# Rows for two products: turned as 16-bit planes by DMA instead of by TensorE

## The chip, the cores and the metric

The kernel runs on one core of a Trainium2 chip. A core has five engines that run side by side, each with its own list of instructions: TensorE (PE) multiplies matrices, VectorE (DVE), ScalarE (ACT) and GpSimd (POOL) work on tiles of 128 partitions, and SyncE (SP) issues transfers (DMA) between DRAM and the on-chip memory, SBUF. TensorE writes its results to a small memory of its own, PSUM, from which DVE or ACT fetch them. An engine works its list in order; where it needs what another engine or a transfer makes, it waits on a semaphore, and everything behind it in its list waits too. ACT and POOL can issue transfers as well.

The metric is the device time of one execution in microseconds (us), smaller is better. It is given as the median of several runs. The profile shows one further execution.

## The reference

A graph of N = 2708 nodes with a feature row of D = 512 numbers each goes through four layers, each followed by `x = layernorm(x + layer(x))`. `adj` is the 2708 x 2708 matrix of edges. Cut to the layers that the change touches:

```python
# layer 0: mean over the first 64 neighbours of every node
keep = Ab & (cumsum(Ab, axis=1) <= 64)
nb_mean = (keep @ X) / max(cnt, 1)
x = layernorm(X + leaky(X @ W_line.T + b_line) + where(cnt > 0, leaky(nb_mean @ W_nb.T + b_nb), 0))
# layer 1: mean over all neighbours
agg = mask @ x / max(deg, 1)
x = layernorm(x + relu(concat([x @ W_self + b_self, agg @ W_nb + b_nb]) @ W_comb + b_comb))
# layer 2: attention with 8 heads; its projection:
Wh = einsum('ni,hio->hno', x, W)        # 512 -> 8 x 64
f1, f2 = Wh . a[:, :64], Wh . a[:, 64:]
# ... softmax over the neighbours, weighted sum of Wh
# layer 3: two more attentions of this kind and a feed-forward part
```

## The kernel before

The rows are worked in 22 tiles of 128 nodes; the last (`LAST`) has 20. The edges lie in SBUF for the whole run as `maskT`, one byte each, transposed, with a sign for kept and other neighbours.

A product `x @ W` on TensorE needs the left operand with the features in the partitions, so each tile of rows is transposed first. `transposed` (lines 132 to 139) does it: four TensorE transposes of 128x128 into one PSUM tile (line 136), and a copy by ACT to the SBUF tile `xT` (line 138). Tiles are drawn ahead of need by `early` (line 161): `early(first, n, make)` makes item i + first when item i is asked for. The row loads are `fetched` (line 174), issued on SP's queue into a ring of three buffers named `rows` in the pool `ahead`. That ring is shared by everything that fetches rows.

The stages that matter here, with the times of the profiled execution:

- 0 to 190 us: layer 0's two products for all tiles, and the first 14 tiles of masks.
- 190 to 455: layer 0's aggregation (lines 571 to 595). Six column blocks of up to four tiles, the short one first; in each, 22 steps in which ACT makes the operand `kT` from the mask (line 444) and TensorE adds into four PSUM banks (line 581). The mean over the neighbours is taken after the product with the weight, here and in layer 1, so `y = x W` is what is aggregated, kept as a high and a low part, `yH` and `yL`. At the end of a block ACT moves the sums out (line 594), and `finish` (lines 494 to 507), drawn a step at a time in the next block, completes the rows of x1: it loads layer 0's second product `r0` and the input row `x0` into `rows` buffers, applies bias, leaky relu and the sum (lines 498 to 504), then the layer norm, which is split between DVE (lines 118 to 125) and POOL (line 123), and stores the row tile to `x1_dram` from POOL's queue (line 506). Beside it the same loop draws steps of `other_masks` (lines 447 to 482: the last eight tiles of masks, each loaded, counted by ACT at line 288, placed by DVE's scans at lines 294 and 297, transposed by an SP transfer at line 315 and written to `maskT` by ACT at line 320), of `weights1` (layer 1's combined weights) and of `vectors` (line 546, the attention's vectors).
- 455 to 620: layer 1's first products (lines 600 to 618). For each tile: fetch the x1 rows, transpose, multiply by the neighbour weight, keep the result as `yH` by ACT (line 242) and `yL` by DVE (line 247), turn a slice of the mask to 0 and 1 by DVE (line 610), multiply by the own weight, add the bias by DVE (line 616), store to `z1_dram`. The steps of `finish` left from the last block are drawn here.
- 620 to 835: layer 1's aggregation (lines 621 to 638): per tile ACT casts mask slices (line 629), TensorE adds over all tiles (line 632), DVE and POOL complete the row of x2 (lines 635 to 637), and POOL's queue stores it (line 638).
- 835 to 927: layer 2's projection, `project` with `source = plain` (lines 705 to 815): per tile fetch the x2 rows, transpose, 16 products (line 759), and the small vectors for the attention that follows.

TensorE's order is that in which the program gives its instructions. On the other engines a planner orders the instructions by costs and due times; `tc.issue_after` holds an instruction behind another.

Of the kernel before, what the change touches and what calls it, by code (L numbers as in the profile page):

```python
# [10 lines left out]
F32 = mybir.dt.float32  # L11
F32R = mybir.dt.float32r
BF16 = mybir.dt.bfloat16
F8 = mybir.dt.float8e4
AF = mybir.ActivationFunctionType
OP = mybir.AluOpType
AX = mybir.AxisListType
# [2 lines left out]
P = 128  # L20
D = 512
KD = D // P
# [9 lines left out]
def kernel(  # L32
# [9 lines left out]
    nc = tc.nc  # L42
    N = x.shape[0]
    NT = -(-N // P)
# [6 lines left out]
    def rows(t):  # L51
        return min(P, N - t * P)
# [7 lines left out]
    dram = ctx.enter_context(tc.tile_pool(name="dram", bufs=1, space=bass.MemoryType.DRAM))  # L60
# [21 lines left out]

    maskT = big.tile([P, NT, NT * P], F8, name="maskT")
    r0_dram = dram.tile([N, D], F32, name="r0_dram")
    x1_dram = dram.tile([N, D], F32, name="x1_dram")
    z1_dram = dram.tile([N, D], F32, name="z1_dram")
    x2_dram = dram.tile([N, D], F32, name="x2_dram")
    x3_dram = dram.tile([N, D], F32, name="x3_dram")


    o_dram = dram.tile([N, D], F32, name="o_dram")
    oT_dram, rc_dram = [], []

# [2 lines left out]
    few = N - (NT - 1) * P  # L96
    LAST, TWIN = NT - 1, 32
# [18 lines left out]
    def layer_norm(pool, y, n, dst, on_scalar=False):  # L116
# [10 lines left out]
        nc.vector.scalar_tensor_tensor(mv[:n, 0:1], mv[:n, 0:1], -1.0, rs[:n], op0=OP.mult, op1=OP.mult)  # L127
        nc.scalar.activation(dst, y, AF.Identity, bias=mv[:n, 0:1], scale=rs[:n])

    copied = []  # L130

    def transposed(pool, psum, src, n, name, order=as_it_comes):

        ps = psum.tile([P, KD, P], F32, name="ps_tr")
        for k in range(KD):
            order(nc.tensor.transpose(ps[:, k, :n], src[:, k * P:(k + 1) * P], ident[:n, :n]))
        dst = pool.tile([P, KD, P], F32, name=name)
        copied[:] = [nc.scalar.copy(dst[:, :, :n], ps[:, :, :n])]  # L138
        return dst

    def transpose_weight(room, psum, dst, src, queues=(nc.sync,)):

# [10 lines left out]
    ahead = fast.enter_context(tc.tile_pool(name="ahead", bufs=2))  # L153
# [7 lines left out]
    def early(first, n, make):  # L161

        made = {}

        def get(i, **how):
            for j in range(len(made), min(i + first + 1, n)):
                made[j] = make(j, **how)
            return made[i]
        return get
# [4 lines left out]
    def fetched(src, t, n, pool=ahead, name="rows", bufs=None, log=None):  # L174
        x_ = pool.tile([P, D], F32, name=name, bufs=bufs or (3 if pool is ahead else None))
        ins = nc.sync.dma_start(x_[:n], src[t * P:t * P + n, :])
        if log is not None:
            log.append(ins)
        return x_[:n]
# [28 lines left out]
    with ExitStack() as phase:  # L208
# [19 lines left out]
        ps_tr = phase.enter_context(tc.tile_pool(name="ps_tr", bufs=2, space=PSUM))  # L228
# [3 lines left out]
        sm = phase.enter_context(tc.tile_pool(name="l01", bufs=2))  # L232
# [53 lines left out]
        def count(i, m):  # L286
            t, n = turns[i], rows(turns[i])
            nc.scalar.activation(m[:n, :N], m[:n, :N], AF.Sigmoid, bias=gate[:n], scale=STEP, accum_out=cnts[:n, t:t + 1])

# [9 lines left out]
        def turn_here(i, m, psum, order=as_it_comes):  # L299
            t, n = turns[i], rows(turns[i])  # L300
            for g0 in range(0, NT, G):
# [6 lines left out]
                for w, a, b in parts:  # L308
                    if a < b:
                        nc.scalar.activation(maskT[:w, a:b, t * P:t * P + n], ps[:w, a - g0:b - g0, :n], AF.Sign,  # L310
                                             saturate=False)
# [12 lines left out]
            b = min(b * P, N)  # L324
            nc.gpsimd.dma_start(maskT[TWIN:TWIN + few, LAST, a * P:b], maskT[:few, LAST, a * P:b])

        def rows_of(src):
            return early(2, NT, lambda t: fetched(src, t, rows(t)))

        with ExitStack() as ph:  # L330
            st = ph.enter_context(tc.tile_pool(name="l0a", bufs=1))
            wnT, wlT = weight(), weight2
            room = [maskT[:, G + k, :4 * D].bitcast(F32) for k in range(2 * KD)]
# [3 lines left out]
            fetches = []  # L337
            xs = early(2, NT, lambda t: fetched(x, t, rows(t), log=fetches))
            xTs = early(0, NT, lambda t, order=as_it_comes: transposed(ahead, ps_tr, xs(t), rows(t), "xT", order))

            warm = sums()
# [5 lines left out]
            xT = xTs(0, order=pe)  # L347
            lows[0] = keep_y(0, P, product(xT, P, wnT, 0, pe))
            xT = xTs(1, order=pe)
# [46 lines left out]
            for t in range(NT):  # L396
                n = rows(t)
# [8 lines left out]
                xT = xTs(t)  # L406
# [17 lines left out]
                u = sm.tile([P, D], F32, name="u")  # L424
# [12 lines left out]
        with ExitStack() as ph:  # L437
# [56 lines left out]
            def finish(ts_, us):  # L494
                for t in ts_:
                    n, u = rows(t), us[t]
                    r0, x0 = fetched(r0_dram, t, n), fetched(x, t, n)
                    nc.vector.tensor_add(u[:n], u[:n], b_nb[:n])
                    leaky(u[:n], u[:n])
                    with tc.issue_after(low.ins):  # L500
                        leaky(r0, r0)
                        nc.vector.tensor_add(r0, r0, x0)
                    yield
                    nc.vector.scalar_tensor_tensor(u[:n], u[:n], has[:n, t:t + 1], r0, op0=OP.mult, op1=OP.add)
                    layer_norm(sm, u[:n], n, u[:n])
                    nc.gpsimd.dma_start(x1_dram[t * P:t * P + n, :], u[:n])
                    yield


# [61 lines left out]
            for i, b in enumerate(cuts):  # L571
# [19 lines left out]
                for t in ts_:  # L591
                    n = rows(t)
# [4 lines left out]
                pass  # L597


            xs = rows_of(x1_dram)  # L600
            xTs = early(0, NT, lambda t: transposed(ahead, ps_tr, xs(t), rows(t), "xT"))
            for t in range(NT):
                n = rows(t)
                xT = xTs(t)
# [10 lines left out]
                u = sm.tile([P, D], F32, name="u")  # L615
# [3 lines left out]
        with ExitStack() as ph:  # L619
            st = ph.enter_context(tc.tile_pool(name="l1b", bufs=2))  # L620
            for t in range(NT):
                n = rows(t)
                x1 = fetched(x1_dram, t, n, st, "x1")
                z1 = fetched(z1_dram, t, n, st, "z1")
                pa = sums()
                for g0 in range(0, NT, G):
                    g1 = min(g0 + G, NT)
                    mf = st.tile([P, G, P], F32R, name="mf")
                    nc.scalar.copy(mf[:, :g1 - g0, :], maskT[:, g0:g1, t * P:(t + 1) * P])  # L629
                    for j in range(g0, g1):  # L630
                        for y in halves(j):
                            nc.tensor.matmul(pa, mf[:, j - g0, :], y(j),  # L632
                                             start=(j == 0 and y is yH), stop=(j == LAST))
                u = sm.tile([P, D], F32, name="u")
                nc.vector.scalar_tensor_tensor(u[:n], pa[:n], rdeg[:n, t:t + 1], z1, op0=OP.mult, op1=OP.add)
                nc.vector.scalar_tensor_tensor(u[:n], u[:n], 0.0, x1, op0=OP.max, op1=OP.add)
                layer_norm(sm, u[:n], n, u[:n])
                nc.gpsimd.dma_start(x2_dram[t * P:t * P + n, :], u[:n])

    late = fast.enter_context(tc.tile_pool(name="late", bufs=1))  # L640
    R2 = late.tile([P, NT, D], F32, name="R2")
# [63 lines left out]
    def project(name, source, layer, v_dram, cuts, turned=None, first=None):  # L705
# [6 lines left out]
        for k in range(KD):  # L712
            for a in range(2):
                src = (w_src[4 * a:4 * a + 4, k * P:(k + 1) * P, :].rearrange("h p o -> p h o") if heads > 1 else
                       w_src[k * P:(k + 1) * P, a * D // 2:(a + 1) * D // 2].rearrange("p (h o) -> p h o", h=1))
                nc.scalar.dma_start(w[:, k, a, :D // 2].rearrange("p (h o) -> p h o", h=hh), src)
        nc.gpsimd.tensor_copy(w[:, :, :, D // 2:D // 2 + heads], wa[:, layer, :, :, :heads])
        with ExitStack() as ph:
            sm = ph.enter_context(tc.tile_pool(name=f"{name}_s", bufs=2))
            ps_tr = ph.enter_context(tc.tile_pool(name=f"{name}_ptr", bufs=2, space=PSUM))  # L720
# [3 lines left out]
            if not first:  # L724
                ps_v, ps_mm = ps_mm, ps_v
            xs = early(1, NT, lambda t: source(sm, t, rows(t)))
            xTs = early(0, NT, lambda t: transposed(ahead, ps_tr, xs(t), rows(t), "xT"))
            if turned:

                cuts_ = [(t, t + 1) for t in range(3)] + [(t, min(t + 2, NT)) for t in range(3, NT, 2)]  # L730
# [1 line left out]
                xTs = lambda t: parts(t if t < 3 else (t - 3) // 2 + 3)[:, :, ((t - 3) % 2 if t > 2 else 0) * P:][:, :, :P]  # L732
# [10 lines left out]
            for t in range(NT):  # L743
                n = rows(t)

                xT = xTs(t)
# [26 lines left out]
                for a in range(2):  # L773
                    to, src = R2[:m, t, a * D // 2:(a + 1) * D // 2], pm[a][:m, :D // 2]
# [42 lines left out]
    class Weights:  # L817
# [45 lines left out]
        def above(self, b, h, j, e, skip=0):  # L863

            w = self.width(b) - skip
            c = self.pool.tile([P, self.W], F8, name="c", bufs=11)
            nc.scalar.activation(c[:, :w], e[:, :w], AF.Sigmoid, bias=bcol[:, j, h:h + 1], scale=STEP, saturate=False)  # L867
# [199 lines left out]
        nc.vector.tensor_scalar(dst, src, 0.0, None, op0=OP.max)  # L1067
        nc.vector.scalar_tensor_tensor(dst, e[:n, :w], -1.0, dst, op0=OP.add, op1=OP.add)  # L1068

    def plain(sm, t, n):  # L1070
        return fetched(x2_dram, t, n)

    def summed(sm, t, n):


# [194 lines left out]
            pass  # L1270

    vd = [dram.tile([heads, N], F32, name=f"v_dram{i}") for i, heads in enumerate((H, H, 1))]
    for i, source in enumerate((plain, summed)):
        with ExitStack() as ph:
            att = Weights(ph, f"a{2 + i}", blocks, vd[i], 5 - i)
            scaled = project(f"p{2 + i}", source, i, vd[i], blocks, first=att.first)
            heads_attention(f"a{2 + i}", att, i == 0, scaled["v"], {
                9 + 4 * t: [lambda t=t: ready.update({t: elu_turned(None, t, t + 1)})] for t in range(3)} if i else {})
# [332 lines left out]
```

## Time and profile before

| What | us |
|---|---|
| median of three runs | 2894.89 (2892.56 to 2897.49) |
| profiled execution, its own time | 2892.55 |
| span of its profile | 2890.8 |
| TensorE busy | 2816.7 |
| DVE busy | 1984.9 |
| ACT busy | 1502.1 |
| POOL busy | 242.2 |
| layer 0's aggregation | 265 (190 to 455) |
| layer 1's first products | 165 (455 to 620) |
| layer 1's aggregation | 215 (620 to 835) |
| layer 2's projection | 92 (835 to 927) |

The span is the time from the first to the last instruction that the profile shows; the execution's own time has 1.75 us around it. The groups of the profile give a line, the engine, the operation, the tiles written and read with their shapes, the count, the busy time, the mean duration in ns, and then the idle time of the engine just before these instructions with what ended it. The granted clock of TensorE was 0.997 of full. Line numbers are those of the kernel before.

### The profile page before, as it was taken

The page shows a single profiled execution, that of the slowest core. Times are in us where ns is not written, and L with a number is a line of the kernel's source. Part 1 is how long each engine was busy: PE and PEld are TensorE (multiplying, and loading weights), DVE is VectorE, ACT ScalarE, POOL GpSimd, SP SyncE. Part 2 cuts the span into 40 slices and gives each one's busy share as a digit, 9 for nine tenths or more (in the row PEclk, how much of TensorE's full clock was granted, in tenths as well). Part 3 has the DMA queues.
Part 4 walks back from the last instruction along what each step waited for, and adds up shares of the span by engine and source line. Part 5 has one row for each costly group of instructions (what it writes and reads, how often), then busy time and mean ns, then how long its engine had stood idle before and what let it go on. Part 6 is the DMA issues. An engine that isn't in the chain of part 4 may idle for free. (4 is left out here: it accounts for less than half of the span.)

```text
span 2890.8 us, 35938 instructions
## 1 busy us (share of the span) xinstructions
PE 2816.7 (97%) x14078; PEld 1568.2 (54%) x14078; DVE 1984.9 (69%) x2344; ACT 1502.1 (52%) x1749; POOL 242.2 (8%) x394
## 2 busy tenths in 40 slices
PE   9999999999999999999999999999999999999998
PEld 5457765458887443444466443444375555554565
DVE  6867837433235999999978999999954435445342
ACT  4646632123224999999955999999950000000011
POOL 2111100101110000000022000000200010100011
PEclk9999999999999999999999999999999999999999
DMA  7745635322222011111152111110161000000000
GB/s 170 153 100 128 164 95 162 108 71 88 81 72 71 28 37 37 35 54 39 36 157 104 37 37 40 50 45 34 36 172 51 4 26 15 26 15 16 15 22 21
DMA packets 162005, 191.65 MB, mean 66 GB/s; under 512 B 82485, under 2 KB 107386, under 8 KB 161826
## 3 DMA queue, kind: packets, MB, share of 16 engines
q1 hardware_dynamic: 132342, 127.59, 15.4%
q0 software_dynamic: 18480, 57.45, 7.0%
q10 hardware_dynamic: 11004, 4.22, 0.6%
q8 instruction: 113, 1.85, 0.3%
q14 instruction: 66, 0.54, 0.1%
HBM read 148.91 MB, written 44.65 MB: 67 GB/s over the span
## 5 line engine op out<-in xcount | busy, mean ns | idle before, releaser
L838 DVE SCALAR_TENSOR_TENSOR e<-v_bc,ucol,maskT 128x1408 f32<-128x1408 f32 (+3 forms) x798 | 1133.5, 1483 | 313.6 <-PE pn L1242 306.6
L867 ACT ACTIVATE c<-e,bcol 128x1300 fp8e4<-128x1300 f32 (+2 forms) x688 | 956.6, 1412 | 61.3 <-DVE e L838 15.9
L1039 PE MATMUL po<-e,R 128*64 128x512 f32 (+3 forms) x4224 | 893.0, 548 | 25.3 <-DVE e L838 23.2
L1039 PEld LDWEIGHTS po<-e,R 128*64 128x64 f32 (+1 forms) x4224 | 333.8, 136 | 551.6 <-issue 390.0
L1242 PE MATMUL pn<-e,R 128*128 128x512 f32 (+1 forms) x1008 | 396.3, 557 | 0.8
L1242 PEld LDWEIGHTS pn<-e,R 128*128 128x128 f32 x1008 | 177.5, 190 | 195.9 <-issue 181.5
L1171 ACT ACTIVATE w<-pl,b 128x256 f32<-128x256 f32 (+1 forms) x88 | 41.0, 466 | 365.6 <-PE pl L1169 365.6
L581 PE MATMUL acc<-yH,kT 128*128 128x512 f32 x418 | 169.9, 407 | 6.7 <-ACT kT L444 4.8
L123 POOL TENSOR_TENSOR ln_rs<-ln_rs,half 128x1 f32<-128x1 f32 (+1 forms) x88 | 55.6, 632 | 1342.4 <-DVE ln_rs L122 1335.2
L759 PE MATMUL pm<-w,xT 128*128 128x264 f32 (+1 forms) x704 | 165.1, 387 | 2.9 <-DVE ln_mv L120 1.2
L581 PE MATMUL acc<-yL,kT 128*128 128x512 f32 x418 | 163.4, 391 | 0.0
L632 PE MATMUL acc<-yH,mf 128*128 128x512 f32 x418 | 162.7, 389 | 0.0
L632 PE MATMUL acc<-yL,mf 128*128 128x512 f32 x418 | 162.6, 389 | 0.0
L1169 PE MATMUL pl<-lin 128*128 128x256 f32 (+1 forms) x704 | 152.9, 371 | 0.6 <-DVE lin L1068 0.6
L1194 PE MATMUL pl<-lin,w 128*128 128x512 f32 x336 | 150.8, 593 | 0.0
L1169 PEld LDWEIGHTS pl<-lin 128*128 128x128 f32 x704 | 129.3, 190 | 31.2 <-issue 15.8
L759 PEld LDWEIGHTS pm<-w,xT 128*128 128x128 f32 (+1 forms) x704 | 129.7, 190 | 25.5 <-ACT xT L138 2.8
L629 ACT CAST mf<-maskT 128x1024 fp32r<-128x1024 fp8e4 (+1 forms) x66 | 64.5, 978 | 151.8 <-PE acc L632 148.2
L270 PE MATMUL pm<-w,xT 128*128 128x512 f32 x288 | 129.8, 593 | 3.7 <-ACT xT L138 2.1
L444 ACT ACTIVATE kT<-maskT 128x512 fp32r<-128x512 fp8e4 (+1 forms) x132 | 77.7, 593 | 102.0 <-PE acc L581 101.7
L939 PE MATMUL pd<-c,parts_c 128*12 128x384 fp8e4 (+2 forms) x2688 | 128.3, 307 | 0.0
L270 PE MATMUL pm<-weight,xT 128*128 128x512 f32 (+1 forms) x256 | 117.0, 600 | 0.6 <-DVE u L616 0.6
(273 smaller groups left out, 2731.7 us busy)
## 6 DMA issues: line engine op xcount, KB each, us to landing
rows<-x_dram SPq DMA_DIRECT2D x63, 256.0 KB
v_bc<-v_dram SPq DMA_DIRECT2D x16, 704.0 KB
rows<-in_x_dram SPq DMA_DIRECT2D x42, 256.0 KB
x_dram<-u POOLq DMA_DIRECT2D x42, 256.0 KB, 2.3
v_bc<-v_dram SPq DMA_DIRECT2D x16, 650.0 KB
m<-in_adj_dram POOLq DMA_DIRECT2D x13, 677.0 KB, 7.3
r_dram<-u POOLq DMA_DIRECT2D x21, 256.0 KB, 3.5
rows<-r_dram SPq DMA_DIRECT2D x21, 256.0 KB
```

Source lines behind the costliest of these rows:

```text
L270: order(nc.tensor.matmul(pm[:m], xT[:, k, :m], w[:, k, :], start=(k == 0), stop=(k == KD - 1)))
L444: made = nc.scalar.activation(kT[:, :w], maskT[:, j, b[0] * P:b[0] * P + w], AF.Relu, scale=-1.0)
L581: nc.tensor.matmul(pa[t], kT[:, (t - b[0]) * P:(t - b[0] + 1) * P], y(j), start=(j == 0 and y is yH), stop=(j == LAST))
L632: nc.tensor.matmul(pa, mf[:, j - g0, :], y(j), start=(j == 0 and y is yH), stop=(j == LAST))
L759: nc.tensor.matmul(pm[a][:m, :D // 2 + heads], xT[:, k, :m], w[:, k, a, :D // 2 + heads], start=(k == 0), stop=(k == KD - 1))
L838: self.made = nc.vector.scalar_tensor_tensor(e[:, :w], v[:, :w], ucol[:, j, h:h + 1], maskT[:, j, c0:c0 + w], op0=OP.max, op1=OP.mult)
L867: nc.scalar.activation(c[:, :w], e[:, :w], AF.Sigmoid, bias=bcol[:, j, h:h + 1], scale=STEP, saturate=False)
L939: pe(nc.tensor.matmul(p[32 * g:32 * g + 12, :c1 - c0], parts_c[:, j, h, :], c[:, c0:c1], start=(i == 0 and h == hs[0]), stop=(i == NT - 1 ...
L1039: pe(nc.tensor.matmul(po[i][HO * k:HO * k + HO, :c1 - c0], R2[at, j, h * HO:(h + 1) * HO], e[at, a:a + c1 - c0], start=(i_ == 0), stop=(i_ ...
L1169: nc.tensor.matmul(pl[:, :w], self.lin1[:, k, f * P:(f + 1) * P], h[:, k, :w], start=(k == 0), stop=(k == KD - 1))
L1194: nc.tensor.matmul(pl[:n], gT[:, f, (t - t0) * P:(t - t0) * P + n], self.lin2[:, f, :], start=(f == 0), stop=(f == KF - 1))
L1242: nc.tensor.matmul(pn[k][:, :w], R2[at, j, k * P:(k + 1) * P], e[at, :w], start=(j == 0), stop=(j == NT - 1))
```

## The change

The transposes of 21 of the 22 tiles in layer 1's first products and in layer 2's projection are taken from TensorE.

When DVE has completed a row tile of x1 or x2, it writes it a second time, as 128x1024 words of 16 bits: first the low halves of the 512 numbers, then the high halves. The room for this copy is a buffer that is done with: `r0` in layer 0 (a buffer of the `rows` ring), `x1` in layer 1. POOL's queue stores the words to a DRAM tensor, `x1_words` or `x2_words`, beside the store of the row itself. Where the tile is needed, one transfer on SP's queue reads the 128x1024 words from DRAM transposed into a `rows` buffer, 8 blocks of 128x128. ACT then interleaves low and high words into `xT`, whose bytes are the transposed 32-bit numbers. The last tile, of 20 rows, goes the old way. The products themselves are unchanged.

```diff
+    x1_words = dram.tile([N, 2 * D], U16, name="x1_words")
+    x2_words = dram.tile([N, 2 * D], U16, name="x2_words")
...
+    def store_words(room, dst, t, u):
+
+        if t == LAST:
+            return
+        words = room.bitcast(U16)
+        nc.vector.tensor_copy(words.rearrange("p (h c) -> p h c", h=2), u.bitcast(U16).rearrange("p (c h) -> p h c", h=2))
+        nc.gpsimd.dma_start(dst[t * P:t * P + P, :], words)
+
+    def turned_words(src, t):
+
+        got = ahead.tile([P, D], F32, name="rows", bufs=3).bitcast(U16).rearrange("p (k n) -> p k n", n=P)
+        nc.sync.dma_start_transpose(got, src[t * P:t * P + P, :])
+        return got
+
+    def joined(words):
+
+        dst = ahead.tile([P, KD, P], F32, name="xT")
+        nc.scalar.copy(dst.rearrange("p k n -> p (k n)").bitcast(U16).rearrange("p (x h) -> p x h", h=2),
+                       words.rearrange("p (h k) n -> p (k n) h", h=2))
+        return dst
+
+    def from_words(words, src, psum):
+
+        got = early(2, NT, lambda t: turned_words(words, t) if t < LAST else fetched(src, t, few))
+        return early(0, NT, lambda t: joined(got(t)) if t < LAST else transposed(ahead, psum, got(t), few, "xT"))
...
                     nc.gpsimd.dma_start(x1_dram[t * P:t * P + n, :], u[:n])
+                    store_words(r0, x1_words, t, u)
                     yield
...
-            xs = rows_of(x1_dram)
-            xTs = early(0, NT, lambda t: transposed(ahead, ps_tr, xs(t), rows(t), "xT"))
+            xTs = from_words(x1_words, x1_dram, ps_tr)
...
                 nc.gpsimd.dma_start(x2_dram[t * P:t * P + n, :], u[:n])
+                store_words(x1, x2_words, t, u)
...
-            xTs = early(0, NT, lambda t: transposed(ahead, ps_tr, xs(t), rows(t), "xT"))
+            xTs = (early(0, NT, lambda t: transposed(ahead, ps_tr, xs(t), rows(t), "xT")) if source else
+                   from_words(x2_words, x2_dram, ps_tr))
```

## The prediction, made before the changed kernel ran

> **What bounds the kernel now.** First the page: its span and the engines.
>
> ```profile
> span 2890.8 us, 35938 instructions
> PE 2816.7 (97%) x14078; PEld 1568.2 (54%) x14078; DVE 1984.9 (69%) x2344; ACT 1502.1 (52%) x1749; POOL 242.2 (8%) x394
> ```
>
> TensorE is busy 97% of the span, so a TensorE instruction that goes away is worth its time unless something else ends last where it stood. The means over the span don't say where that is, so next the stretches of the stages that the change touches (columns: span, then PE, weight loads, DVE, ACT, POOL with counts, clock, DMA share, GB/s): layer 0's aggregation, layer 1's first products (two stretches), its aggregation, layer 2's projection.
>
> ```profile
> 190.00:455.00 265.00, 256.81 (x1052) 191.44 (x1053) 167.44 (x264) 137.94 (x215) 37.27 (x63) 1.00 0.51 126
> 455.00:490.00 35.00, 31.96 (x89) 14.81 (x88) 31.38 (x51) 6.95 (x13) 2.76 (x5) 1.00 0.66 196
> 490.00:620.00 130.00, 128.18 (x358) 58.22 (x356) 65.82 (x80) 22.37 (x40) 15.21 (x27) 1.00 0.28 94
> 620.00:835.00 215.00, 215.00 (x948) 177.71 (x948) 66.69 (x129) 62.43 (x64) 24.45 (x43) 1.00 0.25 80
> 835.00:927.00 92.00, 90.89 (x465) 76.35 (x465) 39.10 (x128) 28.24 (x112) 12.65 (x40) 1.00 0.26 83
> ```
>
> TensorE fills all of them but one: from 455 to 490 DVE is busy 31.4 of 35 us and TensorE idles 3. There DVE still has leftovers of layer 0. Then the groups of the operations concerned:
>
> ```profile
> L629 ACT CAST mf<-maskT 128x1024 fp32r<-128x1024 fp8e4 (+1 forms) x66 | 64.5, 978 | 151.8 <-PE acc L632 148.2
> L136 PE MATMUL ps_tr<-ident,rows 128*128 128x128 f32 (+1 forms) x384 | 57.0, 271 | 3.0 <-ACT rows L128 2.7 <-DMA rows<-in_x_dram 0.3
> L138 ACT COPY xT<-ps_tr 128x512 f32<-128x512 f32 x96 | 54.3, 569 | 22.8 <-PE ps_tr L136 18.7 <-ACT ucol L770 0.6
> L1067 DVE TENSOR_SCALAR lin<-lin 128x512 f32<-128x512 f32 (+1 forms) x24 | 8.4, 390 | 0.0
> ```
>
> Line 136's 271 ns is not the price of a transpose on the path, since matmuls overlap. That is read from the timeline, where four of them begin at 839.85 and the group after them at 840.29:
>
> ```profile
> 839.85 0.60 PE L136 MATMUL ps_tr<-ident,rows 128*128 128x128 f32 x4
> ...
> 840.29 1.95 PE L759 MATMUL pm<-w,xT 128*128 128x264 f32 x8
> ```
>
> So four transposes cost 0.44 us of TensorE (0.43 at 469.26 in layer 1). A whole tile takes 7.31 us in layer 1's products and 4.11 in layer 2's projection. Last, the two starts, where the pipeline is empty, and the transposes by DMA that the kernel already has (duration min/median/max in ns):
>
> ```profile
> 457.69 3.70 PE L270 MATMUL pm<-w,xT 128*128 128x512 f32 x8 [1.43 <-ACT xT L138]
> 465.72 3.70 PE L270 MATMUL pm<-w,xT 128*128 128x512 f32 x8 [0.89 <-DVE yL L247]
> 836.22 3.80 PE L759 MATMUL pm<-w,xT 128*128 128x264 f32 x16 [0.28 <-ACT xT L138]
> L315 SPq DMA_TRANSPOSE weight<-spare x4: 3289/3330/3391, 211.0 to 331.9; - x4
> ```
>
> **What the Trainium skill says.** "DMA: Bandwidth & Descriptors", DMA Transpose (X-bar): the plain transpose goes only through SyncE's and ScalarE's queues, on 2-byte types, into SBUF; hence the planes of words. Line 315 is such a transpose from SBUF; none here reads DRAM. "Advanced Engine Details and Errata", X-Bar Transpose (TRN2): such a transfer is as fast as a plain one, 350 to 400 GB/s: an estimate of 0.7 us for 256 KB. The trace is slower: 128x2816 words (0.72 MB) in 3.33 us is 216 GB/s.
>
> **The change part by part.** It is 21 tiles in each stage; the last, of 20 rows, stays on TensorE.
>
> *Removed.* Two stages x 21 x 0.435 = 18.3 us of TensorE, 42 copies out of PSUM of 0.57 us on ACT, 42 row loads on SP's queue. At layer 2's start the 0.28 us wait goes too. At layer 1's start 2.4 us of transposes and wait lie before the first product, but DVE ends last there (below).
>
> *DVE's word copy,* 42 of 128x1024 words. "VectorE: DVE Perf Modes", Mode 2×_2P: a copy with one source can make two results a cycle in SBUF, if the outermost dimension is even, as it is (2 planes). The trace agrees with that pace for line 1067: 512 in 390 ns, where two-source operations of that size take 0.69 us. 1024 words: 0.65 us at two a cycle (estimate: 0.39 plus 512 more at about 0.5 ns), 1.15 at one (twice line 1067's slope). I take 0.65; 42 x 0.65 = 27 us of DVE. In layer 1's aggregation DVE is busy 67 of 215 us: hidden. In layer 0's aggregation it isn't all hidden.
>
> *POOL's store,* 42 of 256 KB. The row stores there take 0.58 us to issue and 2.3 to land: 24 us of POOL, which is busy 37 of 265 and 24 of 215: hidden, but the landing counts below.
>
> *SP's transposes.* 8 blocks of 128x128 against line 315's 22: 3.33 x 8/22 = 1.2 us (estimate). From below 0.7, the skill's figure; from above 5, if short pieces from DRAM set the pace. Three are in flight ahead of use, and a tile lasts 6.9 and 3.7 us: at 1.2 hidden. If it took over 3.7 us a tile, it would set layer 2's pace.
>
> *ACT's join,* 128x1024 words at stride. Line 629 has that size: 0.98 us; "ScalarE: Activation LUTs", What ACT_TABLE_LOAD costs, prices it at 186 ns + 0.833 per element, 1.04. I take 1.0: +0.43 each over the old copy. ACT in layer 2 goes from 28.2 to 37 of some 83 us: hidden. Joins 0 and 1 stand in ACT's order ahead of layer 0's last casts kT; a late transpose 1 holds kT, and TensorE behind it, by up to 4 us, but mostly in time that DVE will spend anyway.
>
> *Layer 0's aggregation.* Per column block of four tiles DVE gets four copies, 2.6 us, on 34 of 41.5. Worse is the ring of three "rows" buffers: r0's is now the room of the words, and comes free not after line 504 but when the store of the words has landed: copy 0.65 + issue 0.6 + landing 2.3 before the x0 load that follows (2.7 from issue to use). DVE waits for that load at line 502, and behind it on DVE stand the scans of the masks (lines 294, 297), behind these SP's turn (315), ACT's signs (320), ACT's kT (444), and TensorE. I put DVE's loop at 46.8 us a block instead of 41.5. The signs wait hardly at all now: for the turn at 291.3 ACT idles 0.7 us, for that at 331.9 nothing. After two blocks at 5.3 us more each, the turn of 345.0, with 4.2 us of slack, is issued at 355.6; that of 331.9 at about 335.7 only, since the order draws its mask's scans ahead of some copies. ACT stands 3.8 us, TensorE about 3, and then about 2.5 once more: +5.5 us. Lower end 0, if the planner's other order gives the scans room (it puts some earlier than now); upper end +10.
>
> *Layer 1's products.* DVE comes with more left over: the last block's copies and its delayed steps put tiles 0 to 4 some 2 us later, instead of earlier. From tile 5 DVE has 3.0 us of work in 6.87 and TensorE sets the pace: 20 x 0.43 = -8.6. Net -6.5 (from -11.5, when all 21 and the first wait go, to +3).
>
> *Layer 1's aggregation.* Buffer x1 is held until its words have landed, some 4 us more. Two buffers at 9.8 us a tile give 19.4 us and 10.6 are used: nothing. If that cover were gone, 4 us a tile.
>
> *Layer 2's projection.* 21 x 0.44 + 0.28 = -9.3 (from -9.5; the other end is the slow transfer). The attention behind starts earlier by as much: its first loads wait for this stage's end in both kernels.
>
> Sum: +5.5 - 6.5 - 9.3 = -10.3. The profiled execution took 2892.55 us (span 2890.8); the median of the three others is 2894.89, 2.3 above. So 2882.3 in that execution's terms, and 2884.6, say 2885, as a median. With both unknowns at their good end -21: 2874.
>
> **Rivals.**
>
> *All of it gained.* The scans' new places absorb the copies, and DVE at layer 1's start gives nothing back: -18 to -21, 2874 to 2877. For it: TensorE's 97%, the idle 30% of DVE. Against it: DVE's 31.4 of 35 us at the start, and turns that are just in time.
>
> *DVE's chain eats it.* Copies at 1.15 us (+21 us of DVE) or the ring's stalls in layer 0 at +10, layer 1's start at +3: +10 + 3 - 9.3 = +4 at the worst, about 0 in the middle: 2890 to 2899. For it: the turn with no slack. Against it: after 345 no masks are left to place, and from there to 386 DVE is busy only 19.7 of 41 us, so it can catch up.
>
> *Slower: the transpose from DRAM sets the pace.* At layer 2's projection a tile now has 4.11 us. A transpose of s us each, one after another on one queue, gives 20 x (s - 4.11) there once s is above 3.7, while layer 1's tiles (6.87) still hide it. With layer 0's +5.5 and layer 1's -6.5 it breaks even at s = 4.2; at 5 us it is +18 - 1 = +17, 2912. For it: the queue's other transfers, three v_bc loads of 704 KB, stand in the same queue; no transpose here reads DRAM. Against it: line 315's pace from SBUF is a third of that. That the change doesn't remove the transposes at all is out: only the 20-row tile keeps them.
>
> **How the numbers follow.** A measurement can tell 0.2%, 5.8 us, from no change: faster is below 2889.1, slower above 2900.7. Chances: forecast, 2879 to 2889, 0.37; all gained 0.18; eaten 0.24, of which 0.18 within 0.2%, 0.01 faster and 0.05 slower; slow transposes 0.21, all slower. So faster 0.56, same 0.18, slower 0.26. The range 2874 to 2908 leaves out the slowest transposes and gains beyond -21. The likeliest case's own is 2879 to 2889.
>
> **What would show it.** Right: layer 2's tile 3.67 us and layer 1's 6.87 from tile 5; DMA_TRANSPOSE on SP near 1.2 us; the copy near 0.65, the join near 1.0; new TensorE waits for kT at about 336 to 360, with ACT standing for the transposed mask. Wrong: a copy above 1 us; waits of ACT's join for the transposes all through layer 2 (the slow rival); no wait in layer 0 (all gained); waits for DVE in layer 1 beyond tile 5.

## The result

| | before | after |
|---|---|---|
| median | 2894.93 us (2892.56 to 2897.49) | 2901.65 us (2900.3 to 2908.35) |
| ratio | 1 | 1.0028, 95% interval 1.0015 to 1.0041 |
| profiled execution, its own time | 2892.55 | 2901.70 |
| its span | 2890.8 | 2899.6 |

The changed kernel is slower by 0.28%, 6.7 us. Each median is of six executions; the profiled one lies at the low end of them before and near the median after. The forecast was 2885: the time lies in the stated range, but on the other side of no change.

The stretches of the kernel after, cut at its own stage ends (columns as in the table shown of before):

```profile
190.00:486.00 296.00, 266.87 (x1053) 196.74 (x1053) 180.29 (x284) 139.50 (x217) 50.76 (x80) 0.97 0.52 131
486.00:521.00 35.00, 32.09 (x76) 13.88 (x75) 31.74 (x53) 9.70 (x13) 4.07 (x7) 1.00 0.71 187
521.00:641.50 120.50, 118.65 (x288) 50.68 (x286) 65.52 (x79) 31.15 (x38) 16.12 (x30) 1.00 0.39 106
641.50:856.00 214.50, 214.50 (x947) 177.47 (x946) 81.12 (x150) 64.79 (x66) 35.79 (x64) 1.00 0.35 108
856.00:939.50 83.50, 81.94 (x380) 67.30 (x378) 37.96 (x128) 35.87 (x109) 12.59 (x40) 1.00 0.39 85
```

Layer 0's aggregation takes 296 us where it took 265; TensorE has the same work in it (1053 weight loads in both), and its clock is 0.97 where it was 1.00. The other stages are shorter or the same. Exactly, between the starts of the first and last matmuls of the stages, and with what the prediction's sum gave:

| | before | after | difference | forecast |
|---|---|---|---|---|
| layer 0's aggregation | 265.2 | 295.8 | +30.6 | +5.5 |
| layer 1's products | 165.3 | 155.8 | -9.5 | -6.5 |
| layer 1's aggregation | 214.4 | 214.3 | 0 | 0 |
| layer 2's projection, to the attention's first product | 92.2 | 83.6 | -8.6 | -9.3 |

At the attention's first product the kernel is 12.7 us behind (939.64 against 926.90), at the end of DVE's last instruction 13.8 (2893.4 against 2879.6). What follows that instruction is the last store and the program's end, the same in both kernels: it takes 6.2 us after and took 11.2 before. These 5.0 us are no work of the change; among the kernels of this study the end takes 5.8 to 7.3 us in some and 11.2 to 14.7 in others, and what decides it stays open. Small differences of the medians below have to be read with this in mind.

The groups of the new operations, in the kernel after:

```profile
L161 ACT COPY xT<-rows 128x1024 uint16<-128x1024 uint16 x42 | 48.7, 1160 | 65.4 <-PE pm L299 51.9 <-DMA rows<-x_words 7.2 <-PE pm L787 5.7
L149 DVE COPY rows<-u 128x1024 uint16<-128x1024 uint16 x21 | 14.8, 705 | 0.3
L150 POOL DMA_DIRECT2D x_words<-rows x21 | 12.1, 574 | 2.0 <-issue 1.5 <-DVE ln_rs L125 0.2
```

And the transposes, as the view of their line gives them (duration min/median/max in ns, first and last start in us):

```profile
L155 SPq DMA_TRANSPOSE rows<-x_words x42: 1231/1278/3062, 457.7 to 917.2; - x42
```

Each is near what was put in the sum: copy 0.70 us (0.65), join 1.16 (1.0), transpose 1.28 (1.2), issue of the store 0.57 (0.58). Two of the prediction's prices were read from means that mix tile sizes: at the full size line 1067 takes 0.42 us for 512 numbers, not 0.39, and line 629 1.05 for 1024, not 0.98. The join waits for a transpose 7.2 us in all, four times. No operation is dear; what costs is the order in which they wait for each other.

**Where layer 0's 31 us go.** TensorE's waits in the stage, before and then after (engine, line, for whom; us in total, times, longest):

```profile
PE acc L581 <- ACT kT L444: 6.2, 10, 1.6
PE acc L581 <- ACT u L594: 1.9, 3, 0.6
```

```profile
PE acc L608 <- ACT kT L470: 22.9, 16, 6.8
PE ps_tr L139 <- DMA rows<-in_L_gnn_W_self_dram: 4.8, 1, 4.8
PE acc L608 <- ACT u L621: 1.3, 2, 0.6
```

They are 29.0 us after and were 8.1 before. ACT makes kT. Ahead of kT in its order stand the signs of the masks (the writing to `maskT`), and these wait for the turn, SP's transposing transfer of a mask. Before and after:

```profile
ACT maskT L320 <- DMA weight<-spare: 2.5, 2, 1.9
```

```profile
ACT maskT L349 <- DMA weight<-spare: 12.8, 3, 8.6
ACT maskT L349 <- DMA weight<-w: 9.5, 2, 5.2
```

The turns are late because of SP's queue. SP from 262 us in the kernel before and then after:

```profile
262.15 3.36 SPq L315 DMA_TRANSPOSE weight<-w  x1
265.56 0.57 SPq L176 DMA_DIRECT2D rows<-in_x_dram  x1
...
303.62 3.37 SPq L315 DMA_TRANSPOSE weight<-w  x1
```

```profile
262.52 3.35 SPq L344 DMA_TRANSPOSE weight<-w  x1
278.53 0.33 SPq L205 DMA_DIRECT2D rows<-in_x_dram  x1
...
317.85 3.59 SPq L344 DMA_TRANSPOSE weight<-w  x1
```

The load of x0 that went out at 265.6 now goes out at 278.5. SP's waits in 262 to 282, kernel after:

```profile
SPq L205 <- DMA x_words<-rows: 13.4, 2, 12.6
```

12.6 us in one wait for the landing of a store of words. DVE and POOL show what fills it (r0's last reader is line 530):

```profile
264.71 1.41 DVE L530 SCALAR_TENSOR_TENSOR u<-u,has,rows 128x512 f32<-128x512 f32 x2
...
270.84 0.81 DVE L149 COPY rows<-u 128x1024 uint16<-128x1024 uint16 x1
```

```profile
268.33 0.74 POOL L312 DMA_DIRECT2D w<-in_adj_dram  x1 [0.31 <-DVE ln_mv L123]
...
272.02 0.74 POOL L150 DMA_DIRECT2D x_words<-rows  x1
```

Between the last use of r0 and the copy lies the layer norm, with its trip to POOL: 5.4 us for this tile, 3.2 to 7.0 for the four of this block. From the store's issue at 272.02 to the load at 278.5 are 6.5 us (the four landings of words in this block take 3.8 to 6.4). A mask load of 677 KB was issued from the same queue at 268.33; that it holds the stores up is likely, but was not shown alone. DVE then stands for x0 (L528 at 281.30, after 5.16 us of idling), the scans behind it, and the turn behind these: the turn that was issued at 303.6 comes at 317.9, that of 345.0 at 368.7.

**The clock is part of it.** At each of its four waits over 3 us in this stage TensorE's granted clock goes to half for a while; the kernel after, at the longest wait:

```profile
353.75 5.28 PE L608 MATMUL acc<-end,kT 128*128 128x512 f32 x12 [6.78 <-ACT kT L470]
```

Twelve such matmuls took 3.0 us at 300.1, here 5.28. The clock is at half in four stretches, 20.5 us together (from 324.5, 351.8, 375.7 and 389.4), of which TensorE works in some 16.5: an estimate of 8 us lost. In all TensorE is busy 266.9 us instead of 256.8, 10.1 more for the same work. With 29.0 - 8.1 = 20.9 us more of waits that is the 31.

### The profile page after: what moved, and what is told of

The parts are those of the page before. It is cut to its first block, busy times and chain, and to the rows that moved or that the text cites. A ratio compares the mean times of both kernels' runs of the same rounds, so it can differ in the third digit from the quotient of the medians.

```text
span 2899.6 us, 35696 instructions
## 1 busy us (share of the span) xinstructions
PE 2810.6 (97%) x13910; PEld 1556.4 (54%) x13910; DVE 2009.6 (69%) x2386; ACT 1525.3 (53%) x1749; POOL 269.2 (9%) x436
## 5 line engine op out<-in xcount | busy, mean ns | idle before, releaser
L895 ACT ACTIVATE c<-e,bcol 128x1300 fp8e4<-128x1300 f32 (+2 forms) x688 | 956.7, 1412 | 61.5 <-DVE e L866 16.5
L1194 PEld LDWEIGHTS pl<-lin 128*128 128x128 f32 x704 | 129.3, 190 | 31.2 <-issue 15.8
```

The lines of the kernel that those rows point to most:

```text
L1194: nc.tensor.matmul(pl[:, :w], self.lin1[:, k, f * P:(f + 1) * P], h[:, k, :w], start=(k == 0), stop=(k == KD - 1))
```

## The experiments

Each ratio is to runs of the kernel before beside it on the same chip. "Stage" is layer 0's aggregation, 265.2 us before, and "products" layer 1's, 165.3; the unchanged stages of `p2_only` differ by +1.2 and +2.1 from these (its profile is of the slowest of its 14 executions), so a difference of 2 or 3 us of one profile is nothing.

| run | median | ratio (95%) | stage | products |
|---|---|---|---|---|
| p2_only | 2889.26 | 0.9979 (0.9970 to 0.9987) | +1.2 | +2.1 |
| l1_only | 2922.71 | 1.0098 (1.0081 to 1.0115) | +31.2 | -7.6 |
| store_only | 2935.41 | 1.0135 (1.0119 to 1.0152) | +28.7 | +11.0 |
| copy_only | 2919.36 | 1.0086 (1.0069 to 1.0103) | +22.6 | +1.8 |
| copy_xT | 2898.75 | 1.0017 (1.0010 to 1.0024) | +1.8 | +3.3 |
| xT_room | 2903.93 | 1.0026 (1.0017 to 1.0036) | +14.8 | +7.9 |
| x0_room | 2906.36 | 1.0043 (1.0026 to 1.0059) | +30.7 | -8.9 |
| sp_store | 2914.96 | 1.0074 (1.0057 to 1.0091) | +30.4 | -6.4 |
| late_tiles | 2890.08 | 0.9981 (0.9974 to 0.9988) | +3.0 | -2.1 |
| early_tiles | 2914.08 | 1.0058 (1.0040 to 1.0077) | +21.5 | +0.3 |
| w2_room | 2891.60 | 0.9990 (0.9981 to 0.9999) | +18.5 | -7.7 |
| mix | 2888.00 | 0.9975 (0.9964 to 0.9985) | +17.0 | -7.8 |

**One half at a time.** `p2_only`, against the kernel after:

```diff
-                    store_words(r0, x1_words, t, u)
...
-            xTs = from_words(x1_words, x1_dram, ps_tr)
+            xs = early(2, NT, lambda t: fetched(x1_dram, t, rows(t)))
+            xTs = early(0, NT, lambda t: transposed(ahead, ps_tr, xs(t), rows(t), "xT"))
```

> Only layer 2's half of the change: x2 stored as words, its projection from turned words; layer 1's products as before. In the changed kernel the stretch from the end of layer 1's aggregation to the attention's start is 8.6 us shorter than before, and layer 1's aggregation is as long as before. If the parts are independent: 2895 - 8.6 = about 2886 (2883 to 2889). If the words' copies and stores of x2 cost something that the stage ends didn't show: 2890 or more.

Measured 2889.3, 0.9979, some 6 us faster, just past the slow end of what was expected. Layer 2's half gains what was forecast, less some 2 us. Nothing of it costs anything in layer 1's aggregation (214.3 us).

`l1_only`, against the kernel after:

```diff
-                store_words(x1, x2_words, t, u)
...
-            xs = early(1, NT, lambda t: source(sm, t, rows(t)))
-            xTs = (early(0, NT, lambda t: transposed(ahead, ps_tr, xs(t), rows(t), "xT")) if source else
-                   from_words(x2_words, x2_dram, ps_tr))
+            xs = early(1, NT, lambda t: source(sm, t, rows(t)) if source else fetched(x2_dram, t, rows(t)))
+            xTs = early(0, NT, lambda t: transposed(ahead, ps_tr, xs(t), rows(t), "xT"))
```

> Only layer 1's half: x1 stored as words in r0's buffer, layer 1's products from turned words; layer 2 as before. The stage ends of the changed kernel give +31.0 for layer 0's aggregation and -9.6 for layer 1's products: 2895 + 21 = about 2916 (2911 to 2919).

Measured 2922.7, above the expected range. In the profile 23.6 us of the loss are in the two stages, and the program's end takes 13.5 us, 2.3 more than before and 7 more than in the kernel after. The whole loss is layer 1's half.

**The copy, the store or the reader.** `store_only` is `l1_only` with layer 1's products reading as before; `copy_only` also leaves out the store, by

```diff
-        nc.gpsimd.dma_start(dst[t * P:t * P + P, :], words)
+        if dst is not None:
+            nc.gpsimd.dma_start(dst[t * P:t * P + P, :], words)
...
-                    store_words(r0, x1_words, t, u)
+                    store_words(r0, None, t, u)
```

> The kernel before, with the words of x1 copied and stored from r0's buffer, and read by nothing; all transposes on TensorE as before. Theory ring: the loss comes from r0's buffer being held until the store has landed, so layer 0's aggregation is about 31 us longer without any reader: 2923 to 2928. Rival reader: the turned reads on SP's queue, and the joins on ACT, near the end of that stage carry a good part of it: then under 2915.

> As store_only, but the words are only copied by DVE into r0's buffer and not stored; the buffer comes free with the copy. Theory ring: the landing is missing, so little is lost, 2895 to 2901, and SP waits for no landing. Rival copy: DVE's 21 copies of 0.69 us, ahead of the scans in DVE's order, are what makes the turns late: then 2915 or more.

Without any reader the stage is 28.7 us longer, so the reader is out. The whole, 2935.4, is above what was expected, since the products, still on TensorE, lose 11 us more: TensorE's waits in them, most for DVE, are 11.1 us instead of 4.8, and its clock is at half for 10.2 us. The turned reads give this back in the kernel after. `copy_only` was a miss for the theory as first put, and in the range of its rival: with no store at all the stage is still 22.6 us longer. SP's waits for the last user of r0's buffer, before (line 504) and in `copy_only`:

```profile
SPq L176 <- DVE u L504: 11.8, 12, 2.7
```

```profile
SPq L206 <- DVE rows L149: 47.7, 13, 7.6
```

SP waits 47.7 us for the copy itself (line 149), the new last use of r0's buffer. So it could be DVE's 21 copies, or the hold of the buffer up to them.

**The hold or DVE's time.** `copy_xT` is `copy_only` with another room:

```diff
-                    store_words(r0, None, t, u)
+                    store_words(ahead.tile([P, KD, P], F32, name="xT").rearrange("p k n -> p (k n)"), None, t, u)
```

> As copy_only (2919, layer 0's aggregation 23 us longer than before), but the words are copied into an xT buffer, which is idle for most of this stage, not into r0's; nothing is stored or read. DVE does the same 21 copies. Theory hold: copy_only loses because r0's buffer is now held past line 530 to the end of the layer norm and the copy, and the next tile's x0 load waits for it; without that hold the stage is within 6 us of before, 2895 to 2902. Rival copy: DVE's time and place in its order is the cause: 2912 or more again.

DVE makes the same copies and the stage is 1.8 us longer instead of 22.6; the turn that comes at 366.3 in `copy_only` is at 352.5 (345.0 before). SP's wait for the last user of r0's buffer (line 531 here), and SP at the place where it stood 13 us in the kernel after:

```profile
SPq L206 <- DVE u L531: 16.7, 11, 2.7
```

```profile
265.06 3.32 SPq L345 DMA_TRANSPOSE weight<-w  x1
268.43 0.57 SPq L206 DMA_DIRECT2D rows<-in_x_dram  x1
```

So it is the hold, and not DVE's time for the copies. One reserve: the planner also orders DVE's instructions differently in the two kernels, and how much of the 20 us came through that order was not separated.

**Other rooms with the store.**

`xT_room` is the kernel after with the words in an xT buffer (the edit of `copy_xT`, with `x1_words` as destination), `x0_room` with `store_words(x0, x1_words, t, u)`, and `sp_store` with r0 as room and the store on `nc.sync`.

> The changed kernel whole, with the words of x1 made in an xT buffer instead of r0's. Theory hold: both the hold to the copy and the wait for the store's landing leave the rows ring; layer 0's aggregation falls from +31 to under +6, layers 1 and 2 keep their -9.6 and -8.6: 2878 to 2886. Rival copy: 2895 or more. Rival store (POOL's queue and the DMA engines are what the stores load): 2890 or more, with copy_xT near before.

> The changed kernel with the words of x1 in x0's buffer instead of r0's. The ring of three then holds back r0 of the tile after next, not x0 of the next. Theory hold: most of the +31 goes, but not all, since r0 also is needed for the loop: 2880 to 2893. Rival copy: about as the changed kernel, 2897 to 2904.

> The changed kernel with the words of x1 stored from SP's queue instead of POOL's, where a 677 KB load of a mask row stands ahead of them; room as in the changed kernel. Theory hold: the landing gets some 2 us shorter per tile, but r0's buffer is held as long as in copy_only, and SP now waits for the copy itself: 2892 to 2903. If the queue behind the mask load were the main part: under 2888.

All three missed. `xT_room` frees the rows ring, and its last two turns come at 335.7 and 352.0, about 2 us later after the stage's start than in `copy_xT`; but the joins and layer 1's weights need the xT buffers too. ACT's joins wait 4.0 us in the stage and 19.8 in the products for words to land out of xT buffers. At the stage's end kT stands behind such a join in ACT's order: TensorE waits 4.9 us for it, and its clock is at half for 10.2 us. In the products TensorE waits for the join:

```profile
PE pm L299 <- ACT xT L161: 9.7, 3, 4.9
```

and the clock there is 0.95. So a part of the stall moved from one ring into another. But the result is also what the expectation gave for its rival, the stores (2890 or more with `copy_xT` near before): the stage is 13 us longer than in `copy_xT`, and what of these the stores cost by themselves was not separated from the joins. `x0_room` holds back r0 of a later tile, and SP, which issues in order, stands for it with the x0 load behind it (26.2 us for landings of words up to 400 us, and 48.3 for line 530): the same 30.7 us. `sp_store` exchanges most of SP's wait for landings (16.1 us up to 400, where the kernel after has 49.7) for a wait of SP's own queue for the copy (42.0), and was 13 us slower than the kernel after, of which only some 3 are in the two stages and the rest in later ones and at the program's end. Since it brings a wait of its own, it doesn't measure the landing alone; nearest to that comes `store_only` against `copy_only`, which differ by the store of x1's words alone: 28.7 - 22.6 = 6.1 us of the stage.

**Which blocks.** `late_tiles` and `early_tiles` let only some tiles of layer 1 go by words:

```diff
-                    store_words(r0, x1_words, t, u)
+                    if t in range(8, 16):
+                        store_words(r0, x1_words, t, u)
...
-            xTs = from_words(x1_words, x1_dram, ps_tr)
+            xTs = from_words(x1_words, x1_dram, ps_tr, range(8, 16))
```

(`from_words` uses the old way for the other tiles; `early_tiles` has `(*range(8), 20)` in both places.)

> The changed kernel, but in layer 1 only tiles 8 to 15 go by words; their rows are completed after the last mask has been turned. The other tiles of layer 1 use TensorE; layer 2's half is whole. Theory mask chain: holding r0's buffer costs only where scans and turns of masks stand behind it in DVE's and SP's order; so layer 0's aggregation is within 5 us of before, 8 tiles save 3.5 and layer 2 saves 8.6: 2882 to 2889. Rival any block: the hold costs in every block, since the loads of layer 1's weights use the same ring: 2893 or more.

> The complement: in layer 1 only tiles 0 to 7 and 20 go by words, all completed while masks are still placed and turned; layer 2's half is whole. Theory mask chain: nearly the whole loss of 31 us in layer 0's aggregation is here, at least 20: 9 tiles save 3.9, layer 2 8.6, so 2902 to 2914. Rival any block: about half the loss, 2895 to 2900.

The same hold of the same buffer costs 3.0 us of the stage for the 8 tiles completed after the masks, and 21.5 for the 9 completed beside them. In `early_tiles` ACT's waits for the turns are there again, 22.7 us; in `late_tiles` 4.7:

```profile
ACT maskT L349 <- DMA weight<-spare: 12.3, 3, 8.3
ACT maskT L349 <- DMA weight<-w: 10.4, 2, 5.4
```

```profile
ACT maskT L349 <- DMA weight<-spare: 4.7, 2, 3.0
```

So most of the loss is the mask chain's; 6 of the 30.6 us are in neither of the two kernels. `early_tiles` came out at the upper edge of what was expected and `late_tiles` 1 us above it.

**Towards a better version.**

```diff
-                    store_words(r0, x1_words, t, u)
+                    store_words(weight2.rearrange("p k c -> p (k c)")[:, -D:] if t < 8 or t == 20 else r0, x1_words, t, u)
```

is `w2_room`; `mix` has r0 as room for tiles 8 to 15, an xT buffer for 0 to 7 and 20, and TensorE for 16 to 19.

> The changed kernel whole, but the words of tiles 0 to 7 and 20 are made in the idle last 2 KB a partition of weight2, one buffer, not in r0's; later tiles as in the changed kernel. Nothing is held in the rows ring while masks are turned. Theory mask chain: 2880 to 2891. Against it, a new wait: DVE's copy of one tile waits for the landing of the one before (about 4 us), which for tiles completed in pairs stands in DVE's order ahead of the scans: then 2895 to 2905.

> Layer 2's half whole; in layer 1 tiles 0 to 15 and 20 go by words, 16 to 19 (completed while layer 1's products run) by TensorE. The words of tiles 8 to 15 are made in r0's buffer, those of the others in an xT buffer, which nothing else uses while masks are turned. Theory mask chain: layer 0's aggregation within 6 us of before, as in late_tiles and copy_xT; 17 tiles save 7.4, layer 2 8.6: 2880 to 2886. If the stores themselves (POOL's issue and the DMA engines beside the mask loads) cost in the mask blocks without any hold of the rows ring: 2888 or more.

Both beat the kernel after by over 10 us, and the kernel before by 0.1% and 0.25%, but 17 to 18.5 us of the stage's loss are still there. In their profiles they are not ahead of the kernel before at all: at the attention's first product they are 0.7 and 0.4 us behind it, at DVE's last instruction 0.3 ahead and 1.6 behind. Their gain is the program's end, 6.1 and 5.8 us instead of 11.2. `late_tiles` is 7.3 us ahead at the attention, but its program's end takes 14.3. In `w2_room`, 0.6 us above the expected range, DVE waits 5.9 us for its own earlier stores, as feared. In `mix` the last two turns are at 337.7 and 354.1 (331.9 and 345.0 before), and TensorE waits 13.9 us for kT and 5.5 for layer 1's weights, whose loads stand in the rows ring; the joins, which stand in ACT's order ahead of kT, wait 6.4 us for their transposes. The expected 2880 to 2886 was missed; a cost of the stores beyond the hold is likely, and was not measured alone. `mix`, `p2_only` and `late_tiles` can't be told apart (0.9975, 0.9979, 0.9981 with overlapping intervals). Of these `p2_only` is by far the simplest.

## Why the prediction was wrong

*Layer 2's projection*, -9.3: right, -8.6, and as argued: with the transposes gone TensorE fills the stage (81.9 of 83.5 us), DMA transposes keep pace (1.28 us), ACT's longer copy is hidden. The slow rival (a transpose over 3.7 us) did not occur.

*Layer 1's products*, -6.5 in a range from -11.5 to +3: right in sign, -9.5. TensorE's waits in the stage are as long as before (4.8 and 4.9 us), so the 2 us that DVE's leftovers were to cost did not come; likely TensorE's stalls before it gave DVE the time, which was not tested alone. In `store_only`, with like stalls and TensorE's transposes, the products took 11 us longer than before, so beside those stalls the turned rows are worth more than the 9.1 us of TensorE they free.

*Layer 0's aggregation*, +5.5 with an upper end of +10: this term turned the sign; it measured +30.6. The mechanism was put down link by link (ring, x0 load, line 502, scans, turn, signs, kT, TensorE), and each link shows in the trace. What failed is the size of one term, in the step that sized the hold of r0's buffer: it "comes free not after line 504 but when the store of the words has landed: copy 0.65 + issue 0.6 + landing 2.3". From line 504 (530 in the kernel after) to the landing is not 3.6 us but some 13 in the block looked at, since

- the layer norm lies between line 504 and the copy, with POOL's step and the second tile's work in DVE's order: 5.4 us there (3.2 to 7.0 in the block) that the sum left out. `copy_only`, which has no landing at all, is +22.6 in the stage with this part and the copy;
- the landing was put at 2.3 us, the median of the 42 row stores of both layers. The 18 in layer 0's aggregation had taken 3.3 in the median, up to 6.6, in the trace before; the words take 3.8 to 6.4 in the block.

SP's queue stands 12.6 us for it, and the turns come 14 us later after one block (317.9 against 303.6) and 24 after two (368.7 against 345.0), where 10.6 after two was forecast.

*The clock* was missing altogether: TensorE came back from its long waits at half clock, an estimated 8 of the 31 us.

The rival "DVE's chain eats it" had the right place, but its upper end, 2899, rested on the same +10 and is passed too. The rival's other half, copies at 1.15 us, is refuted (0.70), and `copy_xT` shows that DVE's time was not what mattered. That the range held the result is luck: its upper end came from a rival (a slow transpose) that had nothing to do with it.

*The sum's base*: 12.7 us behind at the attention, 13.8 at DVE's last instruction, became 6.7 in the medians, because 5.0 us less went into the program's end and the profiled execution of before was 2.4 us under its median.

## What to carry to other kernels

When a buffer of a small ring is given a second use, count its hold from the old last reader to the new one, with everything that stands between them in the engines' orders, and not just the new operations; then ask whose load stands behind it in an in-order queue. Before borrowing a buffer beside a chain of work that is just in time, look for a stage without such a chain: here the same edit gained 6 us where the longer hold was hidden (layer 2), and lengthened the stage by over 20 where masks were being turned.

## What the runs showed of the hardware

- In the kernel after, each wait of TensorE over 3 us in layer 0's aggregation (3.1 to 6.8) went with a stretch of half clock of 3.4 or 6.8 us. After the wait of 3.3 us the matmuls started every 0.43 us instead of every 0.23; after that of 6.8 us 12 took 5.28 us instead of 3.0. In the kernel before, three waits of 1.4 to 1.6 us at 202 to 218 us were not followed by half clock; in `p2_only` three of 1.5 to 1.6 were, for 3.4 us from 222. How long a wait must be stays open.
- DMA transposes from DRAM of 128x1024 words took 1.28 us in the median (1.23 to 3.06), in line with the 3.33 us for 128x2816 from SBUF: 205 GB/s against 216.
- ACT's copy with 2-byte elements read and written at stride took 1.16 us for 1024 a partition, where the cast of the same size (line 629) takes 1.05 in the kernel before.
- DVE's copy that takes words apart, two planes of 512, took 0.70 us, near the 0.65 estimated from line 1067's pace and far from the 1.15 at half of it, in spite of the stride.
